# One pipeline over tiles for the last layer of a Perceiver-like stack, and its ternary weight signs made earlier (Trainium2, one core)

## The chip, the cores and the metric

The kernel runs on one core of one Trainium2 chip. A core has five engines that run side by side and meet only through semaphores: TensorE (PE, matmuls, with a queue of its own for weight loads, PEld), VectorE (DVE), ScalarE (ACT), GpSimd (POOL) and SyncE (SP), which issues most DMAs here. The metric is the device time of one execution in microseconds (us); lower is better.

## The reference, cut to what matters

The input x has 128 sequences of 32 tokens with 128 channels, so 4096 rows of 128. Four layers L0 to L3 are applied one after another; each has a cross-attention-like step, an attention-like step and a feed-forward step, and each step is added to x after a layer norm:

```python
x = x + _L2_ffn_ref(_layernorm(x, axis=-1), ...)     # attention over the 128 sequences, and experts
x = x + _L3_xattn_ref(_layernorm(x, axis=-1), ...)   # h @ W_in + a scan over the context ("depool")
x = x + _L3_attn_ref(_layernorm(x, axis=-1), ...)    # 16 heads of 8 channels over the 32 tokens of a sequence
x = x + _L3_ffn_ref(_layernorm(x, axis=-1), ...)     # 128 -> 512 -> 128, relu, weights rounded to -1, 0, 1
```

In `_L3_attn_ref`, scores are `q k / sqrt(8) + rel_bias`, then softmax, values and an output projection. In `_L3_ffn_ref` both weight matrices are replaced by their signs where their magnitude is over a threshold that is worked out from the mean magnitude of the whole matrix ("the ternary network's signs"). All arithmetic is in float32.

## The kernel before, in words

The 4096 rows lie in SBUF as eight groups `X[0]` to `X[7]` of four tiles; a tile is 128 rows, which is four sequences of 32 tokens. There are 32 tiles (`NT`) and eight groups (`NG`). Layers L0 to L2 are staged ahead; L2's feed-forward step, `L2_ffn`, attends over the batch, so it turns the rows around through DRAM: it writes X to `xd`, reads it back as `XB`, works, writes `xe` and reads X back (lines 1586, 1588, 1678, 1680).

`run` loads the weights of `L2_ffn`, `L3_xattn`, `L3_attn` and `L3_ffn` with one DMA each on SP's queue (`weights`, L183). The weights of `L3_ffn` share the buffer `wB` with those of `L2_ffn` and so are loaded after `L2_ffn` is through with them.

`L3` begins with `L3_ffn_signs` (L1876 to L1892): for each of the two matrices a sum of magnitudes on DVE (`a_w`, L1882), a matmul with ones that adds over partitions (`pg`, L1884), thresholds and two passes that make the signs (`lo`, `q`, L1889 and L1891). Then it goes through the groups. For each group there are three pieces of work, written as Python generators that yield at places where other work may be put:

- `xattn13` (L1150): loads `Dg`, takes statistics (`stats`: bn_stats and bn_aggr on DVE, then `rsqrt`, a power on POOL, L218), normalizes on DVE (L224), turns the result with four transposes (`pxt`, L231), multiplies by `W_in` (`ph`, L1163), adds `Dg` to X on POOL (L1166) and `ph` to X on DVE (L237).
- `L3_attn`: statistics again, normalization on ACT (`nb` L1801, `xn` L1804), bias onto X on POOL (L1816), transposes, the projections `pq`, `pk`, `pv` (L1824, L1828, L1835) with their copies `QT`, `KM` (four on ACT) and `V`. Then for each of the four tiles: scores in four buffers `S` of 16 small matmuls (L1844) with the bias added by DVE (L1845), the maximum `m` (L1847), its subtraction on POOL (L1848), the exponential on ACT (L1849), a masked copy of the values `Vb` on POOL (L690), a 32x32 transposition `ET` on DVE (L1854), the values matmuls `po` (L1859), their division by the sum (`nm`, `O`, on DVE), four transposes `pot` (L1866) with a copy `OT` on ACT (L1868), and the output projection `pw` (L1871), which DVE adds to X (L1872).
- `L3_ffn`: statistics, normalization on ACT, transposes, eight records of `ph` (four matmuls of 512 columns, L1907) with relu on ACT, 16 matmuls `po` (L1914), the sum into X and the store to the output (L1918).

A float32 matmul stands as two records in the trace, so a count of 32 `po` or `S` records is 16 matmuls.

The loop runs `xattn13` and `L3_attn` of group `it` `abreast` with `L3_ffn` of group `it - 1`: `abreast` takes steps of the two generators in a fixed proportion (12 to 6). That sets only the order in which the program is written. The order on each engine is then made by a scheduler that lays out instructions by dependence, by priority in the written order and by its own estimate of durations; so before, instructions of all three pieces may stand between each other on TensorE. Where an order is wanted, `queue` (L482) ties each instruction to the one before it on its engine, without any semaphore; `L2_ffn_step` does that for the attention over the batch. Within an engine the order is then final: an instruction that is not ready holds up all that stand behind it.

Working tiles have one buffer (`hs`, `hf`) or two (`ht`, and the PSUM pools `hpm`, `hps`, `hpo`, `hpf`).

Of the kernel before, what the change touches and what calls it, by code (L numbers as in the profile page):

```python
# [9 lines left out]
FP = mybir.dt.float32  # L10
I32 = mybir.dt.int32
U32 = mybir.dt.uint32
AF = mybir.ActivationFunctionType
# [6 lines left out]
NG = 8  # L20
NT = 32
# [136 lines left out]
def abreast(gens):  # L158

    done = [0] * len(gens)  # L160
    live = set(range(len(gens)))
    while live:
        k = min(live, key=lambda k: (done[k] + 1) / gens[k][0])
        done[k] += 1
        if next(gens[k][1], None) is None:
            live.discard(k)


class Kern:
# [1611 lines left out]


    def L3(self, W):
        nc = self.nc
        with self.pool("hq") as hq, self.pool("hs") as hs, self.pool("ht", 2) as ht, self.pool("hf") as hf, \
# [12 lines left out]

# [8 lines left out]

    def L3_attn(self, g, w, ls, lt, lpm, lps, lpo):  # L1810
        nc = self.nc
        rel = w["rel"].rearrange("p (h k) -> p h k", h=H)
        wo4 = w["wo"].rearrange("p (j c) -> p j c", j=4)
# [20 lines left out]
        for i in range(4):  # L1834
            nc.tensor.matmul(ps[:, i], lhsT=xT[:, i * 128:(i + 1) * 128], rhs=w["wqkv"][:, 256:384], start=True, stop=True)  # L1835
        nc.scalar.copy(V[:, :, :, 0:HD], ps)
        yield 1
        for i in range(4):
            E = lt.tile([128, H, T], FP, tag="E")
            for j in range(4):  # L1840
                r = slice(32 * j, 32 * j + 32)
                S = lps.tile([128, 4, T], FP, tag="s")
                for b in range(4):
                    nc.tensor.matmul(S[32 * b:32 * b + 32], lhsT=QT[r, 4 * i + b, :], rhs=KM[r, :, 4 * i + b, :], start=True, stop=True)  # L1844
                nc.vector.tensor_tensor(E[:, 4 * j:4 * j + 4, :], S, rel[:, 4 * j:4 * j + 4, :], ALU.add)  # L1845
            m = lt.tile([128, H], FP, tag="m")
            nc.vector.tensor_reduce(m, E, AX.X, ALU.max)  # L1847
            nc.gpsimd.tensor_tensor(E, E, m.unsqueeze(2).to_broadcast([128, H, T]), ALU.subtract)  # L1848
            nc.scalar.activation(E, E, AF.Exp)  # L1849
            Vb = lt.tile([128, H, 4, HD + 1], FP, tag="Vb")  # L1850
            self.blocked(nc.gpsimd, Vb, V[:, i], HD + 1)
            yield 1
            ET = lt.tile([128, H, T], FP, tag="ET")
            nc.vector.transpose(ET.rearrange("p h t -> p (h t)"), E.rearrange("p h t -> p (h t)"))  # L1854
            ps = lpo.tile([128, 4, 4, HD + 1], FP, tag="o", name="po")
            for k in range(4):
                for j in range(4):
                    h = 4 * j + k
                    nc.tensor.matmul(ps[32 * j:32 * j + 32, k], lhsT=ET[:, h, :], rhs=Vb[:, h], start=True, stop=True)  # L1859
            nm = lt.tile([128, 4, 4], FP, tag="nm")  # L1860
            nc.vector.reciprocal(nm, ps[:, :, :, HD])
            O = lt.tile([128, 4, 4, HD], FP, tag="O")
            nc.vector.tensor_tensor(O.rearrange("p b k d -> p k b d"), ps[:, :, :, 0:HD], nm.unsqueeze(3).to_broadcast([128, 4, 4, HD]), ALU.mult)
            pt = lpo.tile([32, 4, 4, T], FP, tag="o", name="pot")
            for b in range(4):
                nc.tensor.transpose(pt[:, b].rearrange("p j q -> p (j q)"), O[:, b].rearrange("p k d -> p (k d)"), self.ident)  # L1866
            OT = lt.tile([32, 4, 4, T], FP, tag="OT")
            nc.scalar.copy(OT, pt.rearrange("p b j q -> p j b q"))  # L1868
            pw = lpo.tile([128, 128], FP, tag="o", name="pw")
            for j in range(4):  # L1870
                nc.tensor.matmul(pw, lhsT=OT[:, j].rearrange("p b q -> p (b q)"), rhs=wo4[:, j, :], start=j == 0, stop=j == 3)  # L1871
            nc.vector.tensor_tensor(self.X[g][:, i, :], self.X[g][:, i, :], pw, ALU.add)  # L1872
            yield 1


    def L3_ffn_signs(self, w, qw, qpb):  # L1876
# [58 lines left out]
```

## Time and profile before

| | us |
|---|---|
| time, median of 3 runs | 5003.25 (4987.8 to 5008.44) |
| the profiled execution | 5049.65 |
| its span, first to last instruction | 5047.9 |
| TensorE busy in the span | 4255.4 |
| VectorE / ScalarE / GpSimd busy | 3389.1 / 2350.5 / 1292.9 |
| mean granted TensorE clock | 0.885 of full speed |
| stretch of L3, 4693 to 5048 us: TensorE busy | 290.1 of 355 |
| the same stretch: VectorE / ScalarE / GpSimd busy | 162.1 / 126.3 / 148.1 |
| the same stretch: granted clock | 0.72 |

The profile is of one execution, and its times are that execution's. Busy time is the time in which an engine has an instruction running; TensorE's matmuls are pipelined and take longer at a lower granted clock, so a busy TensorE is not one at its peak. The granted clock is what a throttle allowed, as a share of full speed. A wait is put down to what came last before the waiting instruction could start.

### The profile page before, as it was taken

The numbers are of one execution on the slowest core, as the hardware profiler recorded it, in microseconds if no ns is written. First come the engines' busy times: TensorE is split into PE (matmuls) and PEld (weight loads), VectorE is DVE, ScalarE is ACT, GpSimd is POOL, SyncE is SP. The second block draws the span as 40 slices with busy tenths as digits, with TensorE's granted clock in tenths as the row PEclk, the third lists the DMA queues.
The fourth block names the chain that finished last, engine by engine and source line by source line (L and its number), as shares of the span: only waits on it lengthen the run. The fifth ranks groups of instructions, "written<-read, shape, count | busy, mean of one in ns | idle before, by whom it ended". The sixth has DMA issues, their size and how long they took to land. (4 is left out here: it accounts for less than half of the span.)

```text
span 5047.9 us, 90278 instructions
## 1 busy us (share of the span) xinstructions
PE 4255.4 (84%) x33802; PEld 3110.6 (62%) x33802; DVE 3389.1 (67%) x10311; ACT 2350.5 (47%) x6637; POOL 1292.9 (26%) x1309
## 2 busy tenths in 40 slices
PE   7999999999898989875367788988898886879688
PEld 5777676767676766665255565666566653446455
DVE  5336758494948585776645378988898775877444
ACT  4555445454454444422134344545554553763333
POOL 1020211111111102135043522332332323322443
PEclk8999898999999999957588898999999997999677
DMA  4223131314141312245133410010101110000100
GB/s 138 60 59 58 42 63 47 61 42 68 38 73 33 59 49 56 64 99 145 32 99 88 136 44 24 26 33 25 29 28 33 37 42 19 1 1 16 37 12 11
DMA packets 388969, 255.96 MB, mean 51 GB/s; under 512 B 184545, under 2 KB 356961, under 8 KB 388017
## 3 DMA queue, kind: packets, MB, share of 16 engines
q1 hardware_dynamic: 361842, 191.22, 16.2%
q0 software_dynamic: 18240, 58.66, 4.1%
q8 instruction: 267, 4.37, 0.4%
q10 hardware_dynamic: 8448, 0.30, 0.2%
q14 instruction: 172, 1.41, 0.1%
HBM read 211.02 MB, written 39.08 MB: 50 GB/s over the span
## 5 line engine op out<-in xcount | busy, mean ns | idle before, releaser
L218 POOL TENSOR_TENSOR rs<-ve,w_const 128x4 f32<-128x4 f32 (+1 forms) x192 | 190.2, 991 | 1567.4 <-DVE ve L216 1285.8
L544 PE MATMUL S<-cT,q 128*128 128x257 f32 x2048 | 545.2, 406 | 19.3 <-ACT E L548 18.5
L544 PEld LDWEIGHTS S<-cT,q 128*128 128x128 f32 x2048 | 389.7, 200 | 146.9 <-issue 53.9
L546 DVE TENSOR_REDUCE nm<-S 128x1 f32<-128x257 f32 x512 | 214.2, 419 | 337.9 <-PE S L544 336.8
L1389 PE MATMUL S<-cT,QM 128*128 128x289 f32 x1024 | 325.0, 434 | 76.3 <-ACT E L1391 69.7
L548 ACT ACTIVATE E<-S,nm 128x257 f32<-128x257 f32 x512 | 242.7, 475 | 297.5 <-DVE nm L547 296.5
L1391 ACT ACTIVATE E<-S,nm 128x289 f32<-128x289 f32 x512 | 253.7, 500 | 188.8 <-DVE nm L1390 184.7
L724 DVE TENSOR_TENSOR A<-A,elt 128x400 f32<-128x400 f32 (+22 forms) x608 | 290.7, 478 | 4.2
L722 DVE TENSOR_TENSOR elt<-A,row 128x400 f32<-128x400 f32 (+22 forms) x608 | 288.5, 474 | 6.4
L527 PE MATMUL pq<-xT,WQK 128*128 128x128 f32 x2048 | 270.9, 292 | 13.4 <-ACT q L528 13.4
L1389 PEld LDWEIGHTS S<-cT,QM 128*128 128x128 f32 x1024 | 177.0, 197 | 159.0 <-ACT E L1391 69.4
L583 PE MATMUL po<-TA,cN 128*128 128x512 f32 x512 | 270.0, 610 | 4.7 <-DVE xn L224 3.9
L527 PEld LDWEIGHTS pq<-xT,WQK 128*128 128x128 f32 x2048 | 255.5, 202 | 23.7 <-ACT q L528 16.7
L584 PE MATMUL po<-TB,cN 128*128 128x512 f32 x512 | 265.6, 600 | 0.0
L558 ACT ACTIVATE E<-E,sm 128x256 f32<-128x256 f32 x512 | 220.2, 498 | 79.4 <-DVE sm L554 74.5
L241 POOL TENSOR_TENSOR QM<-QT,w_const 128x512 f32<-128x512 f32 x128 | 140.8, 1105 | 438.4 <-PE S L1389 412.9
L1390 DVE TENSOR_REDUCE nm<-S 128x1 f32<-128x289 f32 x512 | 219.9, 449 | 30.0 <-PE S L1389 27.0
L1400 PE MATMUL pt<-w_const,E 128*96 128x128 f32 (+1 forms) x1536 | 235.7, 290 | 0.0
L597 PE MATMUL pout<-WVO,OT 128*128 128x128 f32 x2048 | 234.2, 275 | 0.3 <-ACT OT L585 0.3
L597 PEld LDWEIGHTS pout<-WVO,OT 128*128 128x128 f32 x2048 | 231.7, 192 | 0.9 <-ACT OT L585 0.5
L1400 PEld LDWEIGHTS pt<-w_const,E 128*96 128x96 f32 (+1 forms) x1536 | 182.7, 146 | 61.7 <-issue 37.4
L1721 ACT ACTIVATE E<-S,nm 128x128 f32<-128x128 f32 x512 | 180.3, 399 | 64.5 <-DVE nm L1718 64.5
(526 smaller groups left out, 10351.1 us busy)
## 6 DMA issues: line engine op xcount, KB each, us to landing
cT<-ctxT SPq DMA_DIRECT2D x128, 257.0 KB
cN<-ctx SPq DMA_DIRECT2D x128, 256.0 KB
cT<-ctxT SPq DMA_DIRECT2D x32, 514.0 KB
phik<-PW SPq DMA_DIRECT2D x32, 256.0 KB
phiq<-P SPq DMA_DIRECT2D x32, 256.0 KB
A<-phik SPq DMA_DIRECT2D x128, 64.0 KB
PQ<-phiq SPq DMA_DIRECT2D x32, 256.0 KB
cN<-ctx SPq DMA_DIRECT2D x32, 194.0 KB
```

The lines of the kernel that those rows point to most:

```text
L527: self.follow(st, nc.tensor.matmul(ps[:, k, :, :], lhsT=WQK[:, 4 * j + k, cb * 128:(cb + 1) * 128], rhs=t["x"], start=True, stop=True))
L544: self.follow(st, nc.tensor.matmul(S, lhsT=t["QP"][j][:, cb, b, :, :], rhs=t["cT"][b][:, cb, :], start=cb == 0, stop=cb == 1))
L548: nc.scalar.activation(E[:, j, 0:LK], S, AF.Exp, bias=m, accum_out=sm[:, j:j + 1])
L558: nc.scalar.activation(E[:, j, 0:256], E[:, j, 0:256], AF.Copy, scale=sm[:, j:j + 1])
L583: self.follow(st, nc.tensor.matmul(po, lhsT=cN[:, 0, c], rhs=TA, start=True, stop=False), nc.tensor.matmul(po, lhsT=cN[:, 1, c], rhs=TB, s ...
L584: nc.tensor.matmul(po, lhsT=cN[:, 1, c], rhs=TB, start=False, stop=True))
L597: self.follow(st, nc.tensor.matmul(po[:, 0, :], lhsT=OT[:, cb, h, :, :], rhs=WVO[:, cb, h, :], start=h == 0 and cb == 0, stop=False))
L722: nc.vector.tensor_tensor(t, A[:, k, :, i0:i1].rearrange("p h i -> p i h").unsqueeze(3).to_broadcast([128, m, HC, n]), row[:, :, i0:N].uns ...
L724: nc.vector.tensor_tensor(A[:, i0:i1, :, i0:N], A[:, i0:i1, :, i0:N], t, ALU.subtract)
L1389: self.follow(st, nc.tensor.matmul(S, lhsT=t["QM"][:, 0, 4 * j:4 * j + 4, :], rhs=t["cT"][:, b, :], start=True, stop=True))
L1391: nc.scalar.activation(E[:, j, :], S, AF.Exp, bias=nm[:, j:j + 1], accum_out=sm[:, j, b:b + 1])
L1400: self.follow(st, nc.tensor.transpose(pt[0:n, j * 128:(j + 1) * 128], E[:, j, k0:k1], self.ident))
```

## The change

The signs: the weights of `L3_ffn` get a buffer of their own (`wF`, in the pool `wa`), are loaded with the others ahead of `L2_ffn`, and `L3_ffn_signs` runs there, with two PSUM buffers of its own.

The pipeline: `L3_attn` is cut into a front per group (`L3_attn_front`: statistics, normalization, transposes, projections) and four pieces per tile (`L3_attn_scores`, `L3_attn_values`, `L3_attn_turn`, `L3_attn_end`). The new `L3` steps over tiles. In step n stand the turn of tile n-2, the scores of tile n, the values of tile n-1 and the end of tile n-2, and at four places `side` puts a piece of the next group's front (`side(0)`) or of the FFN of a group whose four tiles are done (`side(1)`). After each piece `order` ties TensorE's instructions into one queue in this written order. The other engines' orders are still the scheduler's. Arithmetic, buffers and instruction shapes are the same.

```diff
-            tags = {"L2_ffn": "wB", "L3_xattn": "wX", "L3_attn": "wA", "L3_ffn": "wB"}
+            tags = {"L2_ffn": "wB", "L3_xattn": "wX", "L3_attn": "wA", "L3_ffn": "wF"}
             with self.pool("wa") as wa, self.pool("wb") as wb:
-                pools = {"wA": wa, "wX": wa, "wB": wb}
+                pools = {"wA": wa, "wX": wa, "wB": wb, "wF": wa}
                 for n in ("L2_ffn", "L3_xattn", "L3_attn", "L3_ffn"):
-                    if n != "L3_ffn":
-                        W[n] = self.weights(pools[tags[n]], n, tags[n])
+                    W[n] = self.weights(pools[tags[n]], n, tags[n])
+                with self.pool("sps", 2, PSUM) as sps:
+                    self.q3 = self.L3_ffn_signs(W["L3_ffn"], wa, sps)
                 self.L2_ffn(W["L2_ffn"])
-                W["L3_ffn"] = self.weights(wb, "L3_ffn", "wB")
                 self.L3(W)
...
     def L3(self, W):
...
-            q = self.L3_ffn_signs(W["L3_ffn"], hq, hpf)
-            for it in range(NG + 1):
-                gens = []
-                if it < NG:
-                    gens.append((12, chain(self.xattn13(it, W["L3_xattn"], hs, hpm), self.L3_attn(it, W["L3_attn"], hs, ht, hpm, hps, hpo))))
-                if it:
-                    gens.append((6, self.L3_ffn(it - 1, W["L3_ffn"], q, hf, hpf)))
-                abreast(gens)
+            q = self.q3
+            w = W["L3_attn"]
+            st, traced = {}, nc.cur_bb.bb.instructions
+            at = len(traced)
+            def order():
+                nonlocal at
+                self.queue(st, *[i for i in traced[at:] if i.engine == nc.tensor.engine])
+                at = len(traced)
+            grp = {}
+            def pro(g):
+                return chain(self.xattn13(g, W["L3_xattn"], hs, hpm), self.L3_attn_front(g, w, hs, ht, hpm, grp)) if g < NG else iter(())
+            new, ffn, fq, units = pro(0), iter(()), [], {}
+            for _ in new:
+                order()
+            def side(k):
+                nonlocal ffn
+                if k == 0:
+                    next(new, None)
+                else:
+                    if next(ffn, None) is None and fq:
+                        ffn = self.L3_ffn(fq.pop(0), W["L3_ffn"], q, hf, hpf)
+                        next(ffn, None)
+                order()
+            for n in range(NT + 2):
+                g, i = n // 4, n % 4
+                if i == 0 and n < NT:
+                    for _ in new:
+                        order()
+                    new = pro(g + 1)
+                if n > 1:
+                    pt = self.L3_attn_turn(units[n - 2], ht, hpo)
+                if n < NT:
+                    units[n] = self.L3_attn_scores(grp[g], i, w, ht, hps)
+                order()
+                side(0)
+                if 0 < n <= NT:
+                    self.L3_attn_values(units[n - 1], ht, hpo)
+                order()
+                side(1)
+                if n > 1:
+                    self.L3_attn_end((n - 2) // 4, (n - 2) % 4, units.pop(n - 2), w, hpo)
+                    if n % 4 == 1:
+                        fq.append(n // 4 - 1)
+                order()
+                side(0)
+                side(1)
+            for _ in ffn:
+                order()
+            while fq:
+                for _ in self.L3_ffn(fq.pop(0), W["L3_ffn"], q, hf, hpf):
+                    order()
...
-    def L3_attn(self, g, w, ls, lt, lpm, lps, lpo):
+    def L3_attn_front(self, g, w, ls, lt, lpm, grp):
...
+    def L3_attn_scores(self, t, i, w, lt, lps):
...
+    def L3_attn_values(self, u, lt, lpo):
...
+    def L3_attn_turn(self, u, lt, lpo):
...
+    def L3_attn_end(self, g, i, u, w, lpo):
...
```

The five new functions hold the statements of the old `L3_attn` in the old order. With the change, line numbers of the pieces become: `pq`, `pk`, `pv` L1867, L1871, L1878; `S` L1891; `po` L1909; `pot` L1919; `pw` L1928; the FFN's `ph` and `po` L1963 and L1970; the signs L1938 to L1947.

More of the change, by code (lines that the diff above doesn't have):

```diff
@@ L1836, in L3_attn @@
         nc.scalar.copy(V[:, :, :, 0:HD], ps)
+        grp[g] = QT, KM, V
         yield 1
-        for i in range(4):
-            E = lt.tile([128, H, T], FP, tag="E")
-            for j in range(4):
[L1841 to L1873, printed above, removed]
@@ new lines, in L3_attn_scores @@
+    def L3_attn_scores(self, t, i, w, lt, lps):
+        nc, (QT, KM, V) = self.nc, t
+        rel = w["rel"].rearrange("p (h k) -> p h k", h=H)
+        E = lt.tile([128, H, T], FP, tag="E")
+        for j in range(4):
+            r = slice(32 * j, 32 * j + 32)
+            S = lps.tile([128, 4, T], FP, tag="s")
+            for b in range(4):
+                nc.tensor.matmul(S[32 * b:32 * b + 32], lhsT=QT[r, 4 * i + b, :], rhs=KM[r, :, 4 * i + b, :], start=True, stop=True)
+            nc.vector.tensor_tensor(E[:, 4 * j:4 * j + 4, :], S, rel[:, 4 * j:4 * j + 4, :], ALU.add)
+        m = lt.tile([128, H], FP, tag="m")
+        nc.vector.tensor_reduce(m, E, AX.X, ALU.max)
+        nc.gpsimd.tensor_tensor(E, E, m.unsqueeze(2).to_broadcast([128, H, T]), ALU.subtract)
+        nc.scalar.activation(E, E, AF.Exp)
+        Vb = lt.tile([128, H, 4, HD + 1], FP, tag="Vb")
+        self.blocked(nc.gpsimd, Vb, V[:, i], HD + 1)
+        return {"E": E, "Vb": Vb}
@@ new lines, in L3_attn_values @@
+    def L3_attn_values(self, u, lt, lpo):
+        nc, E, Vb = self.nc, u["E"], u["Vb"]
+        ET = lt.tile([128, H, T], FP, tag="ET")
+        nc.vector.transpose(ET.rearrange("p h t -> p (h t)"), E.rearrange("p h t -> p (h t)"))
+        ps = lpo.tile([128, 4, 4, HD + 1], FP, tag="o", name="po")
+        for k in range(4):
+            for j in range(4):
+                h = 4 * j + k
+                nc.tensor.matmul(ps[32 * j:32 * j + 32, k], lhsT=ET[:, h, :], rhs=Vb[:, h], start=True, stop=True)
+        nm = lt.tile([128, 4, 4], FP, tag="nm")
+        nc.vector.reciprocal(nm, ps[:, :, :, HD])
+        O = u["O"] = lt.tile([128, 4, 4, HD], FP, tag="O", name="O")
+        nc.vector.tensor_tensor(O.rearrange("p b k d -> p k b d"), ps[:, :, :, 0:HD], nm.unsqueeze(3).to_broadcast([128, 4, 4, HD]), ALU.mult)
@@ new lines, in L3_attn_turn @@
+    def L3_attn_turn(self, u, lt, lpo):
+        nc, O = self.nc, u["O"]
+        pt = lpo.tile([32, 4, 4, T], FP, tag="o", name="pot")
+        for b in range(4):
+            nc.tensor.transpose(pt[:, b].rearrange("p j q -> p (j q)"), O[:, b].rearrange("p k d -> p (k d)"), self.ident)
+        OT = u["OT"] = lt.tile([32, 4, 4, T], FP, tag="OT", name="OT")
+        nc.scalar.copy(OT, pt.rearrange("p b j q -> p j b q"))
+    def L3_attn_end(self, g, i, u, w, lpo):
+        nc, OT = self.nc, u["OT"]
+        wo4 = w["wo"].rearrange("p (j c) -> p j c", j=4)
+        pw = lpo.tile([128, 128], FP, tag="o", name="pw")
+        for j in range(4):
+            nc.tensor.matmul(pw, lhsT=OT[:, j].rearrange("p b q -> p (b q)"), rhs=wo4[:, j, :], start=j == 0, stop=j == 3)
+        nc.vector.tensor_tensor(self.X[g][:, i, :], self.X[g][:, i, :], pw, ALU.add)
```

4 lines of the change are left out of this document (1 added, 3 removed).

## The prediction

> **What bounds the kernel now.** The change touches the last stage, L3, and the seam before it. I read the page first: the span is 5047.9 us and the profiled execution took 5049.65 us, 46.4 us over the median of the three runs (5003.25 us), so differences are worked out inside this execution and then put on the median.
>
> ```profile
> PE 4255.4 (84%) x33802; PEld 3110.6 (62%) x33802; DVE 3389.1 (67%) x10311; ACT 2350.5 (47%) x6637; POOL 1292.9 (26%) x1309
> PE   7999999999898989875367788988898886879688
> PEclk8999898999999999957588898999999997999677
> ```
>
> TensorE leads overall, but its granted clock is lowest in the last three slices, which are L3. So I cut L3 (4693 to 5048 us) into stretches of 10 us; the columns are busy us of each engine, then the granted clock:
>
> ```profile
> core 0: us, PE busy (x) PEld busy (x) DVE busy (x) ACT busy (x) POOL busy (x), PEclk, DMA share, GB/s
> 4730.00:4740.00 10.00, 9.11 (x95) 6.43 (x93) 6.18 (x24) 3.80 (x8) 4.96 (x5) 0.50 0.01 2
> ...
> 4950.00:4960.00 10.00, 8.54 (x25) 4.68 (x26) 4.55 (x26) 4.86 (x12) 5.64 (x6) 0.51 0.01 2
> 4960.00:4970.00 10.00, 9.82 (x130) 5.52 (x129) 4.09 (x13) 6.42 (x11) 6.48 (x6) 1.00 0.01 2
> 4970.00:4980.00 10.00, 9.55 (x168) 7.10 (x167) 6.30 (x21) 3.10 (x5) 3.41 (x4) 1.00 0.04 10
> ```
>
> Two kinds of stretch alternate once per group. In the dense one TensorE does 130 to 168 instructions in 10 us at clock 1.00; in the sparse one 25 at 0.51, and it still looks busy because each matmul takes twice as long. What makes it sparse is one chain of small steps, seen in the timeline (start, length, engine, line):
>
> ```profile
> 4946.44 0.71 PE L1163 MATMUL ph<-w_L_xattn,xT 128*128 128x128 f32 x4
> 4950.14 0.17 DVE L216 TENSOR_SCALAR ve<-mv 128x4 f32<-128x4 f32 x1
> 4950.38 1.02 POOL L218 TENSOR_TENSOR rs<-ve,w_const 128x4 f32<-128x4 f32 x1 [3.12 <-DVE ve L216]
> 4951.68 1.64 ACT L1804 ACTIVATE xn<-X,nb,rs 128x128 f32<-128x128 f32 x4
> 4953.82 1.11 PE L231 MATMUL pxt<-w_const,xn 128*128 128x128 f32 x4
> 4955.61 2.07 PE L1824 MATMUL pq<-xT,w_L_attn 128*128 128x512 f32 x2 [0.68 <-ACT xT L1820]
> ```
>
> From the depool matmul `ph` to the projection `pq` the groups of this profile need 7 to 9.3 us (8.46 here), whatever else runs. No engine but TensorE is near its limit: over 355 us DVE is busy 162, POOL 148, ACT 126, TensorE 290. The waits in L3 (us in total, times, longest) agree:
>
> ```profile
> PE po L1859 <- DVE ET L1854: 18.6, 13, 5.5
> PE pxt L231 <- ACT xn L1804: 10.5, 6, 5.2
> DVE a_w L1882 <- DMA w_L_ffn<-w_L_ffn: 6.3, 1, 6.3
> ```
>
> `pq` starts at 4705.24, 4739.90, 4784.65, 4826.49, 4875.45, 4915.06, 4955.61 and 4992.25 us, and the span ends at 5047.9. So before: 79.4 us from the first `pq` to the third, five periods of 41.5 us (207.6), and 55.65 us after the last: 342.7 us.
>
> **Part 1, the signs.** Before, they stand at the head of L3: DVE waits 6.3 us for the weights and then works from 4682.88 to 4688.85 us, and the first statistics of L3 start at 4688.77. Without them those wait only for X: its load is issued at 4683.84, and the like load `XB` was issued at 4221.01 and used at 4224.03, so 3.0 us, 4686.9: a gain of 1.9 us. Behind L2_attn, DVE is free from 4217.15 to 4224.03 (6.88 us, waiting for `XB`); the built order puts the signs exactly there, and they took 5.97 us, so they cost nothing with 0.9 us to spare. Their two small matmuls follow `pv` (ends 4216.4) on TensorE, which then idles anyway. Their load is one more issue on SP (0.33 us) at about 4151, ahead of the `xd` writes that matter at 4218.58; no later transfer is behind it. Uncovered, all of this would cost up to 6 us. [...]
>
> **Part 2, the pipeline.** It removes no work; it fixes TensorE's order. Per tile n: `pot` of n-2, scores of n, one piece of the next group's front, values `po` of n-1, an FFN piece, `pw` of n-2, two more pieces. In the built order the pieces of a group fall so: in the first tile's step the depool transposes and `ph`; in the second the attention's transposes, `pq`, `pk`, `pv` and the FFN's transposes; in the third four `ph` of the FFN; in the fourth its `po`. Before, `S`, `po` and `pw` were laid between FFN matmuls wherever they were ready; now an unready matmul stops all behind it. Prices at clock 1.00 (0.50): four `pot` 0.6 (1.03), a tile's scores 1.0 plus about 0.5 of waiting, since the third and fourth `S` need a buffer that DVE's add (0.25 to 0.29) frees, `po` values 0.47 (0.71), `pw` 1.15 (2.07), four transposes 0.85 (1.11), depool `ph` 1.4 (2.07), `pq`, `pk` and `pv` 1.0 (2.0) each, FFN `ph` 1.0 each, FFN `po` 4.2 a group.
>
> I walk one period, with 0 at the end of the depool `ph`.
> - DVE's `X+ph` stands behind the transpose ET of the same tile: from values, Vb 1.18, subtract 1.05, exp 0.63, ET 0.71 and hand-overs make 4.0 us, of which `pw` and `ph` cover 2.55. So it runs from 1.4 to 2.1.
> - Then by DVE's order: four score adds 0.98, statistics 0.9, maximum 0.69, aggregates and `ve` 0.57: 5.2. POOL first does the subtract that this maximum released (to 5.55), then the power 1.02: 6.6. nb, and the first of four normalizations on ACT: the transposes start at 7.3. TensorE finished the scores at 2.9 and all else is queued behind: **4.4 us idle**.
> - The transposes are paced by ACT (1.65) to 9.0. The clock is now 0.50: values 9.7, `pw` 11.7, `pq` 13.7, `pk` 15.6, `pv` about 16.3.
> - The FFN's transposes need ACT, which has KM (2.42, from 15.7) and V (0.6) first: normalization from 18.75, transposes 19.3 to 20.9: **3 us idle** again. (POOL's queue would allow 17.5: `X+bo` to 9.8, power, Vb, power, 2.1 of DVE, `X+Dg` 1.27, power.)
> - Rest of the step and the third tile, the clock rising under `ph`: `pot` and scores 23.5, values 24.2, `ph` 27.5, `pw` 28.7, `ph` 30.7. Fourth tile: 0.6+1.5+0.5+2.1+1.15+2.1 = 7.95: 38.6. Next first tile: 0.6+1.5+0.85+0.5+1.15+1.4 = 5.95: **44.5 us**.
>
> This leaves out the clock in the dense part. Before lost it inside dense parts in about half of its groups (0.50 from 4891.2 to 4894.9 and from 4929 to 4935.8, for example), one window of 3.4 us each; a window at half speed costs 1.7 us. FFN matmuls are now spread thinner between attention pieces, so I take one per period: 46.2 us.
>
> [...] In the row 4730:4740 above TensorE is busy 9.11 of 10 us, and the clock stays 0.50; from 4720 to 4739 only attention pieces and transposes ran and it was 0.50 throughout; it rose 3.3 to 5.5 us after `pq`, FFN `po` or FFN `ph` began to run back to back (4875.45 to 4881, 4891.6 to 4894.9, 4955.61 to 4959.6). [...]
>
> Sum after. First to third `pq`: 21.4 us until the second (two tiles' scores and the chain above), then without FFN and at 0.50: projections 6.0, three tiles of 5.6, 3.2 of front, and 11.7 from `ph` to `pq`: 59.1. Five periods: 231. After the last `pq`: 46.2-11.7-2.2 (no further front) = 32.3 to the end of tile 28; then tile 29 with the FFN's wait 8.4, tiles 30 and 31 9.6 and 8.1, the drain of two turns and two `pw` 5.9, and the lone last FFN as before (5028.9 to 5047.9) 19.0: 83.3. Together 373.4 against 342.7: +30.7, less 1.9 for the signs: **+29 us**, 5032 us.
>
> **The rivals.** *Faster: the clock holds.* If the pipeline keeps enough matmuls in every window, TensorE's own 27.3 us a group at 1.00 plus 2 of score waits and the two idle times 7.4 make 36.7; with cold restarts 38.5. That gives about 45 + 5x38.5 + 76 = 313.5, so -31 us: 4972. For it speaks the attention of L2, also in a fixed order, at clock 1.00 with TensorE busy 16.6 of 20 us (4480:4500); against it that its matmuls stream 512 columns, and that the two waits come from DVE, POOL and ACT and do not shrink. It beats before once a period falls under about 39 us.
> *No change: the walk's waits are partly covered.* If `X+ph` is not late and KM does not hold up the FFN's normalization, a period is 42 to 43 us without the lost window; total -5 to +15: about 5009.
> *That the change does not do what it says* is out for the order, which is in the built program; for the signs it would be their 6 us uncovered, inside the range.
>
> **How the numbers follow.** A measurement of this kernel tells about 0.5% (25 us) from no change. Slower as walked, 0.45; the walk with its waits partly covered, within 25 us, 0.35; the clock holds, 0.20. The upper end: a clock that stays at 0.50 in the third tile too adds up to 6 us to each of five periods, 30 us on top of 29, so 5063 with rounding up; more than that gets 1 in 10. The lower end, 4975, cuts the faster case near its middle and leaves out another 1 in 10. The likeliest case's own range is 5028 to 5063.
>
> **What would show it.** Right: in the stretches of after, one hole of over 3 us per group on TensorE ahead of the attention's `pxt`, a second ahead of the FFN's, and clock 0.50 around both; `pq` to `pq` near 46 us; no signs at L3's head, and its first statistics waiting for X instead of following them. Wrong: `pq` to `pq` under 40 us with the clock at 0.9 or more, or no wait of `pxt` for ACT.

## The result, and the profile after

The changed kernel took 5017.45 us (median of 8 runs, 5006.31 to 5029.3), the kernel before 5003.74 us beside it: ratio 1.0032, 95% interval 1.0019 to 1.0044. It is slower by some 14 us. The prediction was 29 us slower, with a range from 4975 to 5063 us that begins under no change; so the direction was right, and the predicted size was about twice the measured one.

The page of the profiled execution after (5006.31 us), the rows that answer to those of before:

```profile
PE 4221.3 (84%) x33802; PEld 3090.9 (62%) x33802; DVE 3391.9 (68%) x10311; ACT 2350.8 (47%) x6637; POOL 1295.3 (26%) x1309
PE   7999999999898999885386698898899877888677
PEclk9999999999999999967687899999999987989677
```

The two profiled executions differ by 43 us in the wrong direction (5049.65 before, 5006.31 after). That lies ahead of the changed stages: the last `pv` of L2 starts at 4216.1 us before and at 4157.3 after. So I compare by stage, from a landmark to the next (the first row is called the seam below, the third the head):

| stage, us | before | after | difference | predicted |
|---|---|---|---|---|
| last `pv` of L2's attention to first statistics of `XB` | 7.95 | 9.52 | +1.6 | 0 |
| from there to the last `py` of L2_ffn | 447.4 | 448.6 | +1.2 | 0 |
| last `py` to first `pq` of L3 | 33.8 | 30.7 | -3.1 | -1.9 |
| first `pq` to third | 79.4 | 58.7 | | 59.1 |
| third `pq` to last | 207.6 | 219.8 | | 231 |
| last `pq` to the end | 55.65 | 79.9 | | 83.3 |
| L3 from its first `pq` | 342.6 | 358.4 | +15.8 | +30.7 |

The five periods from the third `pq` to the last lose 12.2 us. TensorE is busy for 173.9 us of them before and 172.9 after, and idle for 33.7 and 46.9, that is 6.7 and 9.4 us a group: against before, the loss in the periods is idle time of TensorE. The two ends of L3 nearly cancel (20.7 us less ahead of the third `pq`, 24.2 more behind the last).

In L3 `pq` now starts at 4646.1, 4666.0, 4704.8, 4746.8, 4791.4, 4835.9, 4880.3 and 4924.7 us: after a period of 38.9, one of 41.9 and one of 44.7, every 44.4 us. One such group in the trace after, cut where the granted clock changes (columns as before: busy us of each engine, then the clock):

```profile
4839.10:4842.50 3.40, 1.15 (x9) 0.86 (x7) 0.70 (x5) 3.10 (x6) 2.24 (x2) 0.98 0.06 14
4842.50:4856.10 13.60, 12.97 (x88) 6.58 (x89) 3.60 (x11) 5.04 (x10) 5.90 (x6) 0.50 0.05 16
4856.10:4873.20 17.10, 13.42 (x234) 10.13 (x232) 10.57 (x35) 4.16 (x8) 4.43 (x5) 1.00 0.05 17
4873.20:4883.40 10.20, 7.32 (x48) 4.54 (x49) 6.02 (x26) 3.46 (x7) 6.40 (x6) 0.51 0.01 2
```

The clock is full for 20.5 us and half ("cold" below) for 23.9. The chain from the depool `ph` to `pq` in the timeline after (start, length, engine, line; in brackets the idle time and what ended it):

```profile
4823.31 1.16 PE L1163 MATMUL ph<-w_L_xattn,xT 128*128 128x128 f32 x8
4825.29 0.71 DVE L1904 STREAM_TRANSPOSE ET<-E 128x512 f32<-128x512 f32 x1 [1.04 <-ACT E L1896]
4825.92 0.65 DVE L237 TENSOR_TENSOR X<-X,ph 128x512 f32<-128x512 f32 x1
4829.89 1.02 POOL L218 TENSOR_TENSOR rs<-ve,w_const 128x4 f32<-128x4 f32 x1
4831.14 1.65 ACT L1849 ACTIVATE xn<-X,nb,rs 128x128 f32<-128x128 f32 x4 [0.69 <-DVE nb L1846]
4831.69 1.63 PE L231 MATMUL pxt<-w_const,xn 128*128 128x128 f32 x4 [4.24 <-ACT xn L1849]
4842.74 1.61 PE L231 MATMUL pxt<-w_const,xn 128*128 128x128 f32 x4 [2.49 <-ACT xn L1849]
```

`ph` ends at 4824.47; `X+ph` comes after ET, the transposes 7.2 us after `ph`, with TensorE idle for 4.24 us; the last line is the FFN's transposes, 2.49 us idle. These two idle stretches are called the holes below. The waits in L3 after (us in total, times, longest):

```profile
PE pxt L231 <- ACT xn L1849: 50.9, 15, 4.4
PE S L1891 <- DVE E L1892: 25.5, 32, 7.0
```

The wait of `po` for ET (18.6 us before) is gone, and that of `pxt` has grown from 10.5 to 50.9. And the seam behind L2's attention after:

```profile
SPq L183 <- PE pf L1513: 33.1, 1, 33.1
4152.22 1.01 SPq L183 DMA_DIRECT2D w_L_ffn<-w_L_ffn  x1
4162.47 1.28 DVE L1938 TENSOR_REDUCE a_w<-w_L_ffn 128x1 f32<-128x512 f32 x2 [4.05 <-DMA w_L_ffn<-w_L_ffn]
4163.32 3.65 SPq L1588 DMA_DIRECT2D XB<-xd  x8
4166.86 0.48 DVE L200 BATCH_NORM_STATS2 st<-XB 128x6 f32<-128x128 f32 x2
```

DVE waits there for the signs' weights and works on them up to the very start of the statistics. The first line is a wait: SP held the loads of all four weights (the second line is the last of them) until `pf`, a matmul of L2's attention, after a wait of 25.6 us for DVE's `e`. Before, without these waits, the loads went out at 4149.8 to 4150.8. The clock times look alike, but the last `pv` of L2 started 66 to 65 us after the loads before, and 6.5 to 5.1 us after them here.

### The profile page after: what moved, and what is told of

It reads as the page before. It is cut to its first block, busy times and chain, and to the rows that moved or that the text cites. A ratio compares the mean times of both kernels' runs of the same rounds, so it can differ in the third digit from the quotient of the medians.

```text
span 5004.5 us, 90274 instructions
## 1 busy us (share of the span) xinstructions
PE 4221.3 (84%) x33802; PEld 3090.9 (62%) x33802; DVE 3391.9 (68%) x10311; ACT 2350.8 (47%) x6637; POOL 1295.3 (26%) x1309
## 5 line engine op out<-in xcount | busy, mean ns | idle before, releaser
L544 PE MATMUL S<-cT,q 128*128 128x257 f32 x2048 | 544.2, 406 | 20.1 <-ACT E L548 19.3
L527 PEld LDWEIGHTS pq<-xT,WQK 128*128 128x128 f32 x2048 | 254.7, 202 | 23.8 <-ACT q L528 16.7
L1390 DVE TENSOR_REDUCE nm<-S 128x1 f32<-128x289 f32 x512 | 220.2, 449 | 30.6 <-PE S L1389 27.3
```

What stands on the lines that cost most here:

```text
L527: self.follow(st, nc.tensor.matmul(ps[:, k, :, :], lhsT=WQK[:, 4 * j + k, cb * 128:(cb + 1) * 128], rhs=t["x"], start=True, stop=True))
L544: self.follow(st, nc.tensor.matmul(S, lhsT=t["QP"][j][:, cb, b, :, :], rhs=t["cT"][b][:, cb, :], start=cb == 0, stop=cb == 1))
```

## The experiments

My theory after the result (A): pieces stand in the fixed order ahead of the end of their chains, and the two holes, with the cold clock behind them, make the 44.4 us. Rival B: the holes matter little, the clock is low because attention pieces lie between the FFN's. Rival C: single buffers and the chains on POOL and ACT set the period whatever TensorE's order is. Before's median ran from 4991 to 5040 us between the sets of runs, so kernels are compared by their ratio to before in the same set. L2_ffn, which none of them edits, took 447 to 457 us in the 14 profiles (455.2 in e4, whose program is that of after up to L3, with 73 us of it at clock 0.50 against 58), so the stage L3 is read from its own landmarks. A period is the time from `pq` to `pq` between the third and the last. e6, e7 and e8 were timed once each (4910.0, 5063.2 and 5065.4 us, beside medians of before of 4994.8, 5039.6 and 5039.6) and are read from their traces alone.

**e1 and e2: the two parts alone.** e1 is before with the signs early, e2 is after with the signs at L3's head again:

```diff
 # e2, from after
-                with self.pool("sps", 2, PSUM) as sps:
-                    self.q3 = self.L3_ffn_signs(W["L3_ffn"], wa, sps)
                 self.L2_ffn(W["L2_ffn"])
+                W["L3_ffn"] = self.weights(wb, "L3_ffn", "wB")
...
-            q = self.q3
+            q = self.L3_ffn_signs(W["L3_ffn"], hq, hpf)
```

> The kernel before with part 1 alone: signs made ahead of L2_ffn from a buffer of their own, L3 as it was. The traces of before and after give 3.1 us gained at L3's head (last py start to first pq 33.8 to 30.7) and 1.6 us lost behind L2_attn (last pv start to the first XB statistics 7.95 to 9.52). If these two are part 1 and nothing else is, the time is 1.5 us under before, ratio 0.9997, and both seams show the same lengths here. Rival: the signs cost nothing behind L2_attn and the 1.6 us there are chance; then that seam is near 8 us and the time 3 us under before. Second rival: the later places of L3 shift because the scheduler lays L3 out anew; then the time moves by several us either way with the seams unchanged.

> Part 2 alone: the pipeline over tiles, with the signs at L3's head as before. If the parts add up, L3 from its first pq to the end is 358 us as in after (342.6 before) and the time is 15 us over before, ratio 1.003, that is 1 to 2 us over after. The period from pq to pq is 44.4 us in the full groups, with two waits of TensorE in each: 4.2 us ahead of the attention's pxt and 2.5 us ahead of the FFN's. Rival: the early signs are what shifted the clock windows to the steady pattern of after; then the period here is not 44.4 but varies as before (37 to 49).

e1: ratio 1.0007 (0.9996 to 1.0019). L3 takes 342.1 us with the periods of before to 0.3 us, its head 30.65, the seam 8.42; L2_ffn took 454.1 in that profile. e2: ratio 1.0039 (1.0027 to 1.0052), L3 358.8 us, period 44.4, seam 7.59, head 33.9. So the slowdown is the pipeline's, and the early signs neither make nor unmake the pattern. At the seam the twelve kernels with early signs need 8.3 to 10.5 us, 9.0 in the mean, the two without 7.6 and 7.95: a cost of some 1.2 us against a gain of 3.1. The net is under what the times can tell.

**e3 and e4: one kind of piece moved.** The order by step (tile of the group) and place in it (a behind the scores, b behind the values, c and d behind `pw`); F is the front's next piece, N the FFN's:

```diff
 # after, e3, e4
-{(0,a): F, (0,c): F, (1,a): F, (1,c): F, (1,d): N, (2,b): N, (2,d): N, (3,b): N, (3,d): N}
+{(0,a): F, (0,c): F, (2,a): F, (2,c): F, (1,d): N, (2,b): N, (2,d): N, (3,b): N, (3,d): N}
+{(0,a): F, (0,c): F, (1,a): F, (1,c): F, (2,b): N, (2,d): N, (3,b): N, (3,d): N, (0,b): N}
```

> After with one edit: the next group's attention transposes go from the second tile's step to the third's, and pq, pk, pv with them; the FFN's pieces stay. Theory (pieces put in the fixed order before their chains are done make the holes): the chain from ph to xn (7.3 us) is covered by a whole step, so the 4.2 us wait of the attention's pxt goes; KM and V are no longer ahead of the FFN's normalization on ACT, but the FFN's transposes still stand right behind the last pw of their group, whose own chain (add, statistics, power, first normalization) took 3.0 us where nothing else was in the way (4984.54 to 4987.56): one hole of 3 to 3.5 us a group. The period is 27.3 us of TensorE's work at full clock, 2 to 3 of waits for S, the hole and 2 to 3 of cold restart: 34 to 36 us, 40 to 50 us less than after in all, some 30 us under before (ratio 0.994). Rival B (the loss is the FFN's matmuls spread thin, so that the clock stays at 0.50 for half of the time whatever the holes are): period 41 or more, time within 15 us of after. Rival C (the single buffers and the chains on POOL and ACT set the period whatever TensorE's order is): 44 us again.

> After with the other edit: all five FFN pieces half a step later (transposes in the third tile's step behind the values, the last po in the next group's first step), the attention's front as it was. Theory: the FFN's 2.5 us wait goes, the 4.2 us wait of the attention's pxt stays, and the FFN's ph, which raised the clock, come 3 us later, so the cold stretch is as long: period 41 to 44 us, time 3 to 15 us under after (ratio to before 1.000 to 1.003). Rival B: the same as after or worse, period 44 to 46. Rival C: 44 us again.

e3: ratio 0.9961 (0.9947 to 0.9976), L3 321.4 us, periods 37.5 to 37.7 and one of 40.8. Its timeline:

```profile
4880.33 1.15 PE L1929 MATMUL pw<-w_L_attn,OT 32*128 32x128 f32 x8
4887.13 1.63 PE L231 MATMUL pxt<-w_const,xn 128*128 128x128 f32 x4 [5.65 <-ACT xn L1850]
```

The attention's hole is gone, as A said; the FFN's, right behind its group's last `pw`, is 5.65 us, not 3 to 3.5, since DVE has ET and the front's statistics ahead of the FFN's last aggregate, and POOL the front's power ahead of its own. TensorE's waits hardly fell (8.7 us a group against 9.4), yet the period fell by 6.9 us: with one hole instead of two there are 17.1 us at half clock in an even period instead of 23.9, and 20.5 at full clock in both.

e4: ratio 1.0037 (1.0022 to 1.0051); L3 353.6 us, periods 42.3 to 45.0, 43.4 in the mean. The FFN's hole did not go, it moved one piece on, to `ph`: ACT's copy `xT` stands behind the exponential of the tile, and that waits for POOL's subtraction (the text written ahead of e5 put it down to KM and V, which had ended at 4852.9):

```profile
4859.04 0.63 ACT L1897 ACTIVATE E<-E 128x512 f32<-128x512 f32 x1 [4.17 <-POOL E L1896]
4859.58 0.57 ACT L1959 COPY xT<-pxt 128x512 f32<-128x512 f32 x1
4860.20 3.78 PE L1964 MATMUL ph<-xT,q_w 128*128 128x512 f32 x4 [3.79 <-ACT xT L1959]
```

The attention's hole stayed at 4.30 us. The mean period was as A said (41 to 44), but not for A's reason, and the ratio, over A's 1.000 to 1.003, cannot be told from that of after.

**e5 and e6: both moved, and the attention alone.** e5 has `{(0,a): F, (0,c): F, (0,d): N, (1,b): N, (2,a): F, (2,b): F, (2,d): N, (3,b): N, (3,d): N}`. e6 is e5 without L3's feed-forward network:

```diff
     def L3_ffn(self, g, w, q, qs, qpf):
         nc = self.nc
-        mv, rs = self.stats(qs, self.X[g], 4, 1e-5)
-        ...
+        for _ in range(4):
+            yield 1
         nc.sync.dma_start(self.out[g * 512:(g + 1) * 512, :].rearrange("(i p) c -> p i c", p=128), self.X[g])
```

> Both pieces of the fixed order moved, each a whole step or more behind the link that starts its chain: attention transposes and projections in the third tile's step, FFN transposes at that step's end, its ph in the fourth tile's step, its po in the next group's first and second. e3 left one hole of 5.65 us (the FFN's pxt right behind its own group's last pw, 5.6 us of chain), e4 left 4.3 us (attention's pxt) and moved the other from pxt to ph (3.8 us, xT behind KM and V on ACT). Theory: with 7.6 us of TensorE's work between that last pw and the FFN's pxt, and about 10 us between the depool ph and the attention's pxt, no wait over 1.5 us is left; the period is the 30.2 us of work at full clock and 2 to 3 of waits for S, 31 to 35 us; time about 42 us under before (ratio 0.990 to 0.993). Rival B (clock): the pieces of attention between the FFN's hold the clock at 0.50 for a good part although TensorE never waits; then 37 to 40. Rival C (POOL, ACT or single buffers next in line): the holes come back at other pieces, as in e4, and the period stays at e3's 37.5.

> The order of e5 with L3's feed-forward network left out (its statistics, matmuls and sum; X is stored after the attention), so that TensorE gets only the attention's pieces and the next group's front, with TensorE's holes as small as that order can make them. It weighs the clock step of the prediction. By the row of before (busy 9.11 of 10 us at 0.50) and the first groups of after, the granted clock stays near 0.50 from the first group to the last, and the period is 29 to 33 us (32.7 of work at half speed by the rows). Rival: what held the clock down was the holes, not the kind of matmul; then the clock rises after the first group, and the period is 22 to 25 us.

e5: ratio 0.9928 (0.9911 to 0.9946), L3 300.9 us, periods 39.3, then three of 34.1 to 34.2, then 35.3. In four of its full groups, behind the one of 39.3, TensorE waited in all:

```profile
PE S L1892 <- DVE E L1893: 10.0, 16, 1.2
PE pq L1868 <- ACT xT L1864: 4.7, 4, 1.2
PE ph L1964 <- ACT hT L1965: 2.3, 3, 0.8
```

That is 4.3 us a group, none over 1.2; the group of 39.3 has one of 3.6, of the FFN's `ph` for ACT's `hT`. That moving the pieces is enough, as A said, is borne out, and C is out for these orders: TensorE's order alone changed the period. Of B something stays: 10.2 of the 34.1 us are at half clock. Against after, an even group of e5 has 5.1 us less idle time and 13.7 us less half clock. The new order closes the holes and spreads the dense pieces at once, and no run parts the two.

e6 has the same period, 34.1 us, though nearly 9 us of matmuls at full clock (4.0 of `ph`, 4.1 of `po`, 0.7 of transposes in e5) are left out of each group: 27.3 of the 34.1 us are at half clock. It is not free of holes (7.5 us of waits a group, one of 3.7 for S), so a part of the 9 us went into waiting and not into the clock. But this stretch of 14.5 us behind the hole (the second row) has no hole, and nothing in it but the attention's pieces and the front:

```profile
4766.20:4769.60 3.40, 3.40 (x7) 1.56 (x6) 1.93 (x6) 0.96 (x2) 2.62 (x4) 0.50 0.02 5
4780.70:4795.20 14.50, 13.68 (x172) 9.51 (x172) 8.03 (x29) 3.10 (x5) 4.66 (x5) 0.50 0.07 21
```

TensorE is busy 13.68 us of 14.5 and the clock stays at 0.50. The clock changes on a grid of 3.413 us: in the traces of before and after it is 0.50 or 1.00, and from one change to the next is a whole multiple of that length, 3.413 us at the shortest. Two windows of this grid in the stretch, 4783.3 to 4786.7 and 4790.1 to 4793.5, are filled to the end (`pw` and `ph`; `po`, `pw`, `pot` and S), and the next window is at 0.50 all the same. In the first row seven records, of `pq`, `pk` and `pv`, filled 3.4 us, and from 4769.6 it was 1.00. So it is not busy time alone that raises the clock. That is the row 4730:4740 of the prediction again.

**e7, e8 and e12: work added to after.** e7 and e8 compute the last quarter of the FFN's `ph` two and four times; e12 fills the hole ahead of the attention's transposes with three matmuls whose result nobody reads:

```diff
 # e7 (e8: 4)
-            nc.tensor.matmul(ps, lhsT=q["w1"][:, k, :], rhs=xT, start=True, stop=True)
+            for _ in range(2 if k == 3 else 1):
+                nc.tensor.matmul(ps, lhsT=q["w1"][:, k, :], rhs=xT, start=True, stop=True)
 # e12
+                if i == 1 and g + 1 < NG:
+                    pd = hpf.tile([128, 512], FP, tag="f", name="pd")
+                    for _ in range(3):
+                        nc.tensor.matmul(pd[:, 0:384], lhsT=self.ident, rhs=w["wqkv"], start=True, stop=True)
+                    order()
                 side(0)
```

> After with one record more of work per group in the dense part: the last quarter of the FFN's ph is computed twice into the same buffer (one matmul of 512 columns, two records, 1.0 us at full clock by the rows of after). It weighs the prediction's step that a lost clock window is added to a period. The period of after is 44.37 us in three groups running, which is 13 windows of 3.413 us, and the clock pattern repeats. Theory (period and clock windows are locked: work that is added shifts where the windows fall, not the sum): the period stays at 44.4 or jumps to 47.8 (14 windows). Rival (work adds up): 45.4 in each full group, and no fixed clock pattern.

> The same with the quarter computed four times: 3.0 us more work at full clock per group. Theory of the lock: 47.8 us (14 windows) in the groups that follow each other evenly. Rival (work adds up): 47.4 at full clock, so by this dose alone the two are close; it matters together with the single dose, and by whether the clock pattern repeats from group to group.

> After with the hole ahead of the attention's pxt filled: three matmuls of 384 columns whose result nobody reads stand ahead of those transposes (by the rows for 512 columns 0.77 us each at full clock and 1.5 at half, so 2.3 to 4.6 us in a hole of 4.24 us). It parts what the hole costs by itself from what it costs through the clock. Theory 1 (idle time in the hole is what takes the clock away): the clock stays at 1.00 behind the hole in most groups, pw, pq, pk and pv take 4.5 us instead of 8 and the FFN's chain starts that much earlier: period 40 to 42, time about 15 to 25 us under after, ratio to before 0.998 to 1.001. Theory 2 (the attention's small pieces do not hold the clock, hole or no hole, as in the row 4730:4740 of before): the period stays at 44 to 45 and the time within 5 us of after, ratio 1.003 to 1.004.

e7: periods 43.0, 41.4, 43.1, 45.7 and 43.1, L3 359.3 us, 0.9 more than after for 8 us of work. Neither expectation holds: there is no fixed pattern, and the work does not add up. e8: 44.3 to 44.4 in four groups running, the period of after with 3 us more work in it, not the 47.8 that my lock demanded nor the 47.4 of adding up. Its waits for `pxt` and S are those of after to 0.2 us a group, and its clock pays for the work:

```profile
4893.50:4900.40 6.90, 6.46 (x75) 3.38 (x75) 2.12 (x7) 2.16 (x6) 5.63 (x5) 0.51 0.00 0
4900.40:4924.20 23.80, 19.32 (x252) 12.98 (x250) 12.81 (x42) 6.47 (x11) 5.50 (x7) 1.00 0.04 12
```

Half clock for 6.9 us where after has 13.6, full for 23.8 where after has 17.1. What e8 loses in L3, 11.2 us, comes behind the last `pq` (8.9, where two networks with the added work are left and the last runs alone) and in one early period (3.0); the rest of L3 is 0.7 shorter.

e12: ratio 1.0026 (1.0007 to 1.0046), L3 354.8 us, period 44.4 with the clock pattern of after in the last groups. The hole ends when `xn` is there, and the clock fell all the same:

```profile
4820.37 2.20 PE L1827 MATMUL pd<-w_L_attn,w_const 128*128 128x384 f32 x6
4824.68 1.63 PE L231 MATMUL pxt<-w_const,xn 128*128 128x128 f32 x4 [2.11 <-ACT xn L1854]
```

The period is that of theory 2 of that run: filling half of the hole bought nothing in the even periods. But the run does not part the two theories. In the clock windows ahead of the falls at 4780.8, 4825.2, 4866.1 and 4910.5 TensorE was busy for only 1.2 to 1.9 of 3.41 us, since the rest of the hole or the wait for S lies there (0.6 in after). That the attention's pieces do not hold the clock rests on e5 and e6, and a hole that is filled to the end stays untested.

**e11: one term of the walk.** After, with Vb tied behind the subtraction of its tile on POOL:

```diff
+        traced = nc.cur_bb.bb.instructions
+        at = len(traced)
         nc.gpsimd.tensor_tensor(E, E, m.unsqueeze(2).to_broadcast([128, H, T]), ALU.subtract)
         nc.scalar.activation(E, E, AF.Exp)
         Vb = lt.tile([128, H, 4, HD + 1], FP, tag="Vb")
         self.blocked(nc.gpsimd, Vb, V[:, i], HD + 1)
+        self.queue({}, *[x for x in traced[at:] if x.engine == nc.gpsimd.engine])
```

> After with one edit on POOL alone: Vb is tied behind the subtraction of the maximum of its tile (in after it stands ahead of it and takes 1.18 us). It weighs one term of the walk: X+ph stands behind ET, and ET behind values, Vb 1.18, subtraction 1.05 and exp 0.63. If the walk is right, ET and X+ph come up to 1.2 us earlier and the wait of the attention's pxt falls from 4.24 to 3.0 to 3.4 us in every full group. For the time: by adding up, 1 us for each of seven groups, 5 to 8 us under after, ratio to before about 1.002. Rival (the windows of the clock decide): the wait falls as said, but the period stays near 44.4 or becomes uneven, and the time is within 3 us of after, ratio about 1.003. Second rival (ET is not what holds X+ph): the wait stays at 4.2.

Ratio 1.0030 (1.0016 to 1.0045); L3 took 367.0 us in its profile, with periods of 42.4, 44.9, 47.3, 44.9 and 47.3. The wait of S behind ET fell from 1.54 to 0.80 us, so ET and `X+ph` do stand behind Vb; but the hole grew from 4.24 to 5.22:

```profile
4841.72 1.17 POOL L690 TENSOR_TENSOR Vb<-V,w_const 128x576 f32<-128x576 f32 x1
4842.85 1.02 POOL L218 TENSOR_TENSOR rs<-ve,w_const 128x4 f32<-128x4 f32 x1
4844.65 1.63 PE L231 MATMUL pxt<-w_const,xn 128*128 128x128 f32 x4 [5.22 <-ACT xn L1849]
```

The Vb that was tied behind the next tile's subtraction now stands ahead of the power that the hole waits for. I had moved it past one queue entry and not looked at the next.

**e9 and e10: the rest of e5.** e9 puts a piece between the second and third S of each tile (place m): `{(0,m): F, (0,c): F, (1,m): N, (1,d): N, (2,m): F, (2,c): F, (2,d): N, (3,m): N, (3,b): N}`. e10 adds e11's edit and gives Dg's two steps to DVE:

```diff
         for j in range(4):
+            if j == 2:
+                mid()
             r = slice(32 * j, 32 * j + 32)
 # e10 also
-        nc.gpsimd.tensor_tensor(Dg, Dg, w["ginit"].unsqueeze(1).to_broadcast([128, 4, 128]), ALU.mult)
-        nc.gpsimd.tensor_tensor(Dg, Dg, w["b"].unsqueeze(1).to_broadcast([128, 4, 128]), ALU.add)
+        nc.vector.tensor_tensor(Dg, Dg, w["ginit"].unsqueeze(1).to_broadcast([128, 4, 128]), ALU.mult)
+        nc.vector.tensor_tensor(Dg, Dg, w["b"].unsqueeze(1).to_broadcast([128, 4, 128]), ALU.add)
```

> A refinement of e5, to see whether its rest can be had: in e5 the third and fourth S wait 0.4 to 1.2 us in each tile for the add on DVE, and pq 1.2 us for xT. Here one piece is put between the second and third S of each tile (depool transposes, FFN po, attention transposes, FFN ph), and pq, pk, pv go behind pw. Theory (waits first, clock follows): TensorE's waits fall from about 5.3 us a group to under 3, and the period from 34.1 us (10 windows) to 30.7 (9 windows), 15 to 25 us less than e5 in all: ratio to before 0.988 to 0.990. Rival B (clock): the attention's pieces alone keep the clock down for 10 us of each group whatever the waits are: 34.1 us again. Rival C (DVE's order is the bound: adds stand behind the transpose ET, the sums into X and the statistics): the waits come back in other places and the period is 33 to 36.

> e9 with POOL cleared in front of the subtraction of the maximum: Dg's two steps go to DVE, and Vb is tied behind the subtraction of its tile. In e9 one wait was left in each group, 3.9 us (third S behind DVE's add), and its chain is plain in the trace: the subtraction stood on POOL behind Dg's two steps and Vb (4874.0 to 4877.53), so exp, then ET on DVE, and behind ET the adds that free the buffers of S. Theory (the next link of POOL's queue is what held TensorE): the wait goes to under 1 us, the period from 35.1 to 31 or 32 us, L3 from 298.8 to 275 to 282, ratio to before 0.987 to 0.989. Rival B (clock): the clock takes back what the wait gives, as it did with the doses of work in e7 and e8; period 33.5 to 35, ratio 0.991 to 0.992. Rival C (DVE is next): Dg's two steps, about 0.7 us each, and the adds wait in DVE's queue instead; period 34 to 36.

e9: ratio 0.9919 (0.9901 to 0.9937), not to be told from e5; L3 298.8 us, periods 33.9 to 36.2, waits 5.2 us a group. The many short waits became fewer and longer ones, up to 3.91, and the chain of that one starts on POOL (Dg at 4874.00 and 4875.18, then these):

```profile
4876.40 1.17 POOL L690 TENSOR_TENSOR Vb<-V,w_const 128x576 f32<-128x576 f32 x1
4877.53 1.05 POOL L1905 TENSOR_TENSOR E<-E,m 128x512 f32<-128x512 f32 x1
4880.93 0.84 PE L1901 MATMUL S<-KM,QT 32*32 32x128 f32 x16 [3.91 <-DVE E L1902]
```

e10: ratio 0.9899 (0.9882 to 0.9915), L3 294.9 us, periods 31.0 to 35.2, waits 4.0 us a group. It has the lowest ratio of all with the whole network, about 50 us under before, though its interval still meets that of e9; but the period did not fall to 31 or 32, and a wait for S of up to 3.4 us is left. The clock and DVE's order (rivals B and C) may share that rest, and which of the two edits gained what is open; no run parts them.

## Why the prediction was right, and what was mis-sized

- **The mechanism** held: TensorE's fixed order stops all work behind two pieces whose chains end on ACT. Predicted 4.4 and 3 us idle, measured 4.24 and 2.49; predicted transposes 7.3 and 19.3 us after `ph`, measured 7.2 and 18.3. e2 shows the slowdown with the pipeline alone, and e3 and e5 that moving these pieces, and nothing else, takes it away.
- **The walk of one period**, 44.5 us, was measured as 44.4 in three groups running. That it came within 0.1 us is luck: three errors cancel. The FFN's transposes ended 1.0 us earlier than walked (19.9 behind `ph`, not 20.9). From there to the end of the FFN's `ph` took 12.3 us, not 9.8: the walk let the clock rise by the end of the first `ph`, at 27.5, and it stayed at 0.50 to 31.5. The rest, at full clock, took 12.2, not 13.8. From first to third `pq` 59.1 was predicted and 58.7 measured, of which the first part was 19.8 instead of 21.4 and the second 38.9 instead of 37.7. (Before, two of the eight groups needed 21.8 and 10.9 us from `ph` to `pq`, not 7 to 9.3; no sum rests on that.)
- **The mis-sized term is the lost clock window**, 1.7 us added to each of five periods and once in the tail, 10.2 us: no window was lost in the dense part, where the clock was full for five windows running. (Of the two examples for it from before, the second, 4929 to 4935.8, is two windows and not one.) e7 and e8 say why adding it up was wrong in kind: work put into the dense part shifted windows from half to full clock (in e8 6.9 us at half where after has 13.6), so 3 us more of it changed the period by nothing in e8. The rest of the 15 us is a shorter third period (41.9) and 1.7 us of the tail: five periods of 44.5 make 222.5 where 219.8 were measured, the tail without the window 81.6 where 79.9 were.
- **The clock step**, taken from the row 4730:4740, held: the first two groups after, with attention alone, took 58.7 us where the row's prices gave 59.1, with the clock at half for 45 of them, and e6 repeats the row over 14.5 us. Before, the clock also fell, at 4949.54, behind a window that was not idle: TensorE was busy for 1.49 of its 3.41 us.
- **The cases.** The time, 5017 us, lies under the likeliest case's own range (5028 to 5063) and nearer to the second case's 5009. That case's condition, a walk whose waits are partly covered, is not what the trace shows: both waits are there.
- **The signs, at the head.** The gain is 3.1 us, not 1.9: the statistics start 2.9 us after X's load is issued, as predicted (3.0), and that load is itself issued 1.1 us sooner behind the last `py`. Before, the signs' weights are loaded 1.3 us ahead of the `xe` write that X is read back from, and X's load follows that write by 3.2 us; without this load it follows by 2.1. In e2, which has the load there again, it is 3.3, and in the other eleven kernels with early signs 2.1 to 2.2.
- **The signs, at the seam.** The cost behind L2's attention is 1.6, not 0. The step that failed is that the load goes out long ahead of the `xd` write, with "no later transfer" behind it. With the larger pool `wa` SP held all four loads in the two waits named above; the load of the signs' weights left 7.6 us ahead of that write, where those of before had left 68 us ahead of it. DVE waited 4.05 us for it and finished the signs some 0.5 us too late (if `XB` takes the 3.0 us of before), and from the `xd` write to the issue of `XB` it took 3.5 us instead of 2.4. All twelve kernels with early signs have the wait for `pf`, and the cost goes with it: where the load leaves 5.7 to 5.8 us ahead of the last `pv`, the seam is 8.3 to 8.7 us; at 5.1 it is 9.0 to 9.5, and at 4.4 to 4.6 it is 10.0 to 10.5. So in these runs the seam is longer the later the load leaves, and in after the read back is issued 1.1 us later behind the small write than before; by what means is not shown. That SP waits because the larger pool lies over places that L2's attention still uses is inferred from the waits.
- **What would show it**: both holes, half clock around them (but for the window 4838.9 to 4842.3 ahead of the FFN's) and first statistics waiting for X instead of following the signs are in the trace; "`pq` to `pq` near 46" was 44.4.
- **The sum**: L3 +15.8 instead of +30.7, head -3.1, seam +1.6: +14.3, against 13.7 measured between the medians (L2_ffn's +1.2 lies within its scatter of 10).

## What to carry to other kernels

When an order is fixed by hand, place each piece by the length of the chain that feeds it on the other engines, counted from the piece that starts the chain: here a step of 8 us between them turned +0.3% into -0.7%. Then read each engine's queue again, since a piece that is no longer waited for uncovers the next link (`xT` behind the exponential, 3.79 us in e4; the power behind Vb, 5.22 in e11; the subtraction behind Dg, 3.91 in e9). And where the clock changes with the order of the work, as here (23.9 us a period at half clock in after, 17.1 in e3), do not add up work or lost windows by themselves: count the cold time around each hole.

## What I had not expected of the hardware

Dense matmuls were nearly free beside sparse ones: in even groups the network's nearly 9 us cost nothing in e5 against e6 (over all five periods 35.4 against 33.5 us in the mean), and 3 us more cost nothing in e8's period. In e8 the granted clock, which changes on a grid of 3.413 us, paid for them; in e5 the clock and 3.2 us less of waiting did. Evenly repeating groups came out at whole windows (34.1 us for 10, 37.5 for 11, 44.4 for 13), but not of necessity (e7, e10). And the clock can fall without a long hole: in e5 a window in which TensorE was busy 3.01 of 3.40 us with attention pieces (4834.1 to 4837.5) was followed by one at 0.50.
